# The norm's reciprocal root by Ln and Exp on ScalarE, in place of Sqrt on ScalarE and a reciprocal on VectorE

## Chip, cores and metric

The kernel runs on one core of a Trainium2 chip. The metric is the device time of one launch in microseconds, the median of the runs shown. The engines are called PE (TensorE), DVE (VectorE), ACT (ScalarE), POOL (GpSimd) and SP (SyncE, which only issues transfers here).

## What is computed

A layer of 2048 tokens and 1024 channels: a normalised input goes through a Mamba-2 block and, beside it, through a linear layer with a mixture of LoRA experts; both are added to the input. Cut to what matters:

```
xn = layernorm(x)
gate, hbc, dt = split(xn @ in_proj_w.T)
xBC = silu(causal_conv4(hbc))                  # x (64 heads of 64), B, C (8 groups of 128)
state = state * exp(dt * A) + (dt * x) B^T     # per token and head
y = state C + x * D
yg = y.reshape(L, 8 groups, 512)
var = mean(yg * yg, axis=-1)
yn = yg * rsqrt(var + 1e-5) * norm_weight * silu(gate)
out = x + yn @ out_proj_w.T + base(xn) + lora(xn)
```

The change is about `rsqrt(var + 1e-5)`.

## The kernel before

Channels lie on partitions. Tokens are cut into two spans `s` of 1024, each span into two halves of 512 (TB), each half into four chunks of 128 (Q). Large matrix products are done with one or two levels of Strassen's scheme in fp32: one pair of output tiles takes seven products of four 128x512 steps (`pair`, L450), in the order 1, 6, 5, 2, 7, 3, 4 on the PSUM tiles ps_a, ps_x, ps_y, ps_a, ps_x, ps_y, ps_x. Copies and sums between them (L474 and L529 on ACT; L478, L482 and L531 on DVE) take a partial result out of PSUM before the next product may add to the same tile. Product 7's eviction (L531) has to be done before product 4 starts, one product later.

After a start-up, a loop runs over 32 blocks (span, group, half) and in each over four chunks (L974 to L1069). It interleaves the scan with the projections: each chunk draws four or five of the seven products of a pair from a generator (`products`, L591), so that PE always has projection work between the steps of the scan. Matmuls keep their program order; the other engines' instructions are put in order by the framework's scheduler, and each engine then runs its list strictly in order. So an instruction that waits holds up all that stand behind it.

One chunk of the scan: `scan_a` makes the decay products `es` (L688, DVE), then C^T B and B^T (ps_cb), copied out as cbm and bt (L698, L700, ACT), the masked matrix dab (L702, DVE), then x transposed (ps_xt) and scaled to xdt (L713, eight ACT instructions) and xdd (L720, POOL). `scan_b` makes ps_y from xdt and dab, ps_e from the state, ps_st for the next state, and takes them out on DVE (L757 or L759, L760, L774). The tiles ps_cb, ps_xt and ps_nv share one PSUM bank, "aux".

In chunks 1 and 2 of a block, `conv` makes the next block's convolution: a first tap on ACT (L640), three more on DVE (L646), Silu on ACT (L653). Its output tile xg has two buffers, so the first L640 of the next block waits until the block before has stored its last result from the same buffer.

The norm of a block is spread over two blocks. In the last chunk `norm_squares` adds x * D (L793) and squares (L798, ACT). In the first chunk of the following block `norm_mean` (L804) sums over channels with a matmul by ones (ps_nv, L807), ACT takes Sqrt into the tile rms (L809), and `norm_gate` (L812) takes the reciprocal on DVE (L815), multiplies four slices by norm_weight and rms (L818), multiplies by the gate in two halves (L826) and stores each (L827, SP queue). There are 32 such norms.

In the first span, `small` (L297) makes the second span's dt, decay and router weights for four pieces of tokens, in between; its softplus is a chain of short DVE instructions (L319 to L326) that ends in `at` (L329, DVE), of which ACT takes Exp (`ex`, L330).

ACT's functions come from tables; the profile shows each switch as ACT_TABLE_LOAD, put down to the line of the instruction that needs it. Silu is used by L529 and L533 (gate) and L653, Exp by L315, L330, L338 and L385, Sqrt by L225, L268 and L809.

After the blocks comes the output projection with two levels of Strassen (from 2740 us on), in which ACT has little to do.

## Time and profile before

| | |
|---|---|
| Median of 3 runs | 3461.18 us (3456.09 to 3463.89) |
| The profiled execution's own time | 3459.94 us |
| Its span on the core | 3458.2 us |
| TensorE clock granted | 0.996 |
| Span under ACT's work in blocks | about the first 2700 us |

The profile's first part gives each engine's busy time as a share of the span. The waits give, for an engine and line, what released it, with the total in us, how often, and the longest. A group of instructions is told as line, engine, operation, tiles, shapes and count, then the busy time in us, the mean ns of one, and the idle time before it with its releaser. The chain that ended last is read from the end back: start, length, and what ran then; "issue" is time in which the engine waited for nothing that the profile shows, or in which the work of the line above goes on, as for the second piece of a long instruction.

The 40 slices of the span show where each engine works (tenths of each slice):

```profile
PE   9999999999999999999999999999999999999999
PEld 7444544544545554444555555444445588888888
DVE  7548787877887877677888887777885466566665
ACT  2223343333433333323333333333331000000000
```

### The profile page before, as it was taken

The page shows a single profiled execution, that of the slowest core. Times are in us where ns is not written, and L with a number is a line of the kernel's source. Part 1 is how long each engine was busy: PE and PEld are TensorE (multiplying, and loading weights), DVE is VectorE, ACT ScalarE, POOL GpSimd, SP SyncE. Part 2 cuts the span into 40 slices and gives each one's busy share as a digit, 9 for nine tenths or more (in the row PEclk, how much of TensorE's full clock was granted, in tenths as well). Part 3 has the DMA queues.
Part 4 walks back from the last instruction along what each step waited for, and adds up shares of the span by engine and source line. Part 5 has one row for each costly group of instructions (what it writes and reads, how often), then busy time and mean ns, then how long its engine had stood idle before and what let it go on. Part 6 is the DMA issues. An engine that isn't in the chain of part 4 may idle for free.

```text
span 3458.2 us, 37638 instructions
## 1 busy us (share of the span) xinstructions
PE 3409.4 (99%) x12818; PEld 1993.4 (58%) x12818; DVE 2530.2 (73%) x2861; ACT 926.4 (27%) x2158; POOL 832.3 (24%) x571
## 2 busy tenths in 40 slices
PE   9999999999999999999999999999999999999999
PEld 7444544544545554444555555444445588888888
DVE  7548787877887877677888887777885466566665
ACT  2223343333433333323333333333331000000000
POOL 3133323233333211332332433322332000000000
PEclk9999999999999999999999999999999999999999
DMA  6546655655656676787787788787777687585644
GB/s 234 189 164 201 209 178 189 206 191 197 199 193 205 197 262 220 246 283 231 240 251 245 234 260 253 234 255 226 244 233 270 236 279 242 198 299 188 213 165 145
DMA packets 530319, 769.79 MB, mean 223 GB/s; under 512 B 35152, under 2 KB 264656, under 8 KB 527440
## 3 DMA queue, kind: packets, MB, share of 16 engines
q1 hardware_dynamic: 530128, 767.39, 68.6%
q8 instruction: 102, 1.67, 0.2%
q14 instruction: 89, 0.73, 0.1%
HBM read 516.64 MB, written 250.61 MB: 222 GB/s over the span
## 4 chain that ended last, share of the span: by engine, by line
PE 77%; DVE 10%; issue 6%; DMA 4%; POOL 2%; ACT 1%; SPq 0%; POOLq 0%; DVEq 0%; ACTq 0%
PE ps_x_x L79 10%; PE ps_x_w L79 8%; PE ps_a_x L79 7%; PE ps_y_x L79 7%; PE ps_x_g L79 6%; PE ps_a_w L79 6%; PE ps_y_w L79 6%; PE ps_y_g L79 4%; PE ps_a_g L79 4%; PE ps_y L79 3%; PE ps_e L79 3%; PE ps_x_b L79 2%; PE ps_st L79 2%; PE ps_a_b L79 2%; PE ps_y_b L79 2%
## 5 line engine op out<-in xcount | busy, mean ns | idle before, releaser
L688 DVE TENSOR_TENSOR_SCAN es<-dab,here 128x1024 f32<-128x1024 f32 x128 | 327.3, 2557 | 285.8 <-POOL xdd L83 264.6
L83 POOL TENSOR_TENSOR xdd<-xdt,es 128x512 f32<-128x512 f32 x128 | 145.3, 1135 | 1003.4 <-ACT xdt L713 967.6
L646 DVE SCALAR_TENSOR_TENSOR xg<-rawx,cw,xg 128x512 f32<-128x512 f32 x384 | 339.8, 934 | 22.3 <-ACT xg L640 21.7
L79 PE MATMUL ps_x_w<-t,w 128*128 128x256 f32 x1344 | 303.8, 379 | 0.0
L79 PEld LDWEIGHTS ps_x_w<-t,w 128*128 128x128 f32 x1344 | 255.4, 190 | 41.5 <-issue 7.7
L713 ACT ACTIVATE xdt<-ps_xt,dt 128x64 f32<-128x64 f32 x1024 | 223.2, 331 | 201.4 <-PE ps_xt L88 201.4
L83 POOL TENSOR_TENSOR wo<-wo 128x512 f32<-128x512 f32 (+1 forms) x112 | 214.1, 1912 | 16.6 <-DMA ecp<-run_d 10.3
L83 POOL TENSOR_TENSOR state<-state,tot 128x512 f32<-128x512 f32 x112 | 134.5, 1201 | 322.4 <-PE ps_e L79 311.0
L79 PE MATMUL ps_a_w<-q,w 128*128 128x256 f32 x896 | 202.5, 379 | 0.0
L702 DVE TENSOR_TENSOR dab<-es,cbm 128x1024 f32<-128x1024 f32 x128 | 174.1, 1360 | 27.5 <-ACT cbm L698 27.4
L1336 ACT COPY s<-ps_a_w 128x512 f32<-128x512 f32 x28 | 16.4, 585 | 636.2 <-PE ps_a_w L79 568.9
L79 PEld LDWEIGHTS ps_a_w<-q,w 128*128 128x128 f32 x896 | 170.2, 190 | 23.6 <-issue 0.5
L79 PEld LDWEIGHTS ps_y<-dab,xdt 128*64 128x64 f32 x2048 | 114.0, 138 | 109.6 <-issue 72.6
L79 PE MATMUL ps_y_x<-op_again,s_x 128*128 128x512 f32 x384 | 173.3, 594 | 0.0
L79 PE MATMUL ps_x_x<-op_again,s_x 128*128 128x512 f32 x384 | 172.7, 592 | 0.0
L79 PE MATMUL ps_a_x<-op_again,a_x 128*128 128x512 f32 x384 | 172.7, 592 | 0.0
L79 PE MATMUL ps_x_x<-op,s_x 128*128 128x512 f32 x368 | 165.5, 592 | 0.0
L79 PE MATMUL ps_y_x<-op,s_x 128*128 128x512 f32 x368 | 165.5, 592 | 0.0
L79 PE MATMUL ps_a_x<-op,a_x 128*128 128x512 f32 x368 | 165.4, 592 | 0.0
L646 DVE SCALAR_TENSOR_TENSOR bc<-rawb,cw,bc 128x512 f32<-128x512 f32 x192 | 159.1, 859 | 4.0 <-ACT bc L640 3.2
L79 PE MATMUL ps_y<-dab,xdt 128*64 128x128 f32 x2048 | 145.9, 283 | 13.4 <-ACT xdt L713 13.4
L79 PE MATMUL ps_e<-bc,state 128*128 128x128 f32 x960 | 142.1, 292 | 0.0
(236 smaller groups left out, 6050.7 us busy)
## 6 DMA issues: line engine op xcount, KB each, us to landing
w<-w SPq DMA_DIRECT2D x196, 512.0 KB, 3.7
dab<-da_d SPq DMA_DIRECT2D x128, 512.0 KB, 5.1
raw<-ev SPq DMA_DIRECT2D x192, 256.0 KB, 3.2
a_x<-in_w_in_dram SPq DMA_DIRECT2D x168, 256.0 KB, 4.2
w<-wo SPq DMA_DIRECT2D x96, 448.0 KB, 3.5
ecp<-run_d SPq DMA_DIRECT2D x256, 128.0 KB, 4.0
gate<-ev SPq DMA_DIRECT2D x128, 256.0 KB, 3.5
sg<-gate SPq DMA_DIRECT2D x32, 1024.0 KB, 7.3
```

The source lines that it names most:

```text
L79: tc.keep_in_program_order(nc.tensor.matmul(*args, **kw))
L83: ins = nc.gpsimd.tensor_tensor(*args)
L646: nc.vector.scalar_tensor_tensor(dst[:, i, :], raw[:, i, k : k + TB], cw[:, ti, k : k + 1], dst[:, i, :], ALU.mult, ALU.add,)
L688: nc.vector.tensor_tensor_scan(es.rearrange("p h t -> p (h t)"), dab.rearrange("p h t -> p (h t)"), here, 0.0, ALU.mult, ALU.add,)
L702: nc.vector.tensor_tensor(ms, es, cbm.unsqueeze(1).to_broadcast([P, HG, Q]), ALU.mult)
L713: ins = nc.scalar.activation(xdt[:, h, :], x_t[:, h, :], AF.Copy, scale=dt_of[s][:, half * NQ + c, at : at + 1],)
L1336: nc.scalar.copy(s1, pa)
```

## The change

In `norm_mean` the ACT instruction computes Ln(var + eps) in place of Sqrt, from the same PSUM tile, with the same bias and scale. A second ACT instruction then computes Exp(-0.5 * that) in place in the tile rms, in SBUF. The reciprocal on DVE at the head of `norm_gate` is gone; its `yield` stays, so the following steps are handed out at the same points of the program. The other lines are the same; line numbers from L810 on move by one or two.

```diff
         std = p1.tile([P, TB], F32, tag="rms", name=f"rms_{s}_{g}_{half}")
-        nc.scalar.activation(std, ps, AF.Sqrt, bias=eps, scale=1.0 / (4 * P))
+
+        nc.scalar.activation(std, ps, AF.Ln, bias=eps, scale=1.0 / (4 * P))
+        nc.scalar.activation(std, std, AF.Exp, scale=-0.5)
         norm_of[s, g, half] = std
 
     def norm_gate(s, g, half):
 
         xg, std = xbc_of[s, g, half][0], norm_of[s, g, half]
-        nc.vector.reciprocal(std, std)
         yield
```

The two other places that take Sqrt and a reciprocal, the layer norms at L225 and L268, are left as they are. In the new file Ln is L810, Exp L811, and what was L818, L826 and L827 is L819, L827 and L828; the prediction uses the old numbers, except L811 for Exp.

## The prediction

> **What bounds the kernel now.** I read the page's first part (busy time by engine), then who waited for whom on TensorE (PE), then the groups that the change touches, then two stretches of the chain that ended last.

> ```profile
> PE 3409.4 (99%) x12818; PEld 1993.4 (58%) x12818; DVE 2530.2 (73%) x2861; ACT 926.4 (27%) x2158; POOL 832.3 (24%) x571
> ```

> PE is busy in all but 49 us of the 3458.2 us span. VectorE (DVE) and ScalarE (ACT), which the change edits, count only where PE stands still for them. PE's own waits (us, times, longest):

> ```profile
> PE ps_y L79 <- ACT xdt L713: 13.4, 5, 6.8
> PE ps_nv L79 <- ACT xdt L713: 10.0, 4, 2.7
> PE ps_st L79 <- POOL xdd L83: 5.4, 1, 5.4
> ...
> PE ps_x_g L79 <- DVE ev L531: 2.7, 4, 1.3
> PE ps_mean L79 <- DVE half L183: 1.7, 2, 1.5
> PE ps_x_x L79 <- DVE ev L531: 1.7, 4, 0.6
> ```

> The whole list sums to 43.5 us: the ceiling of any gain, 1.3%. ps_y behind xdt lies almost wholly at four places: PE starts ps_y at 451.69, 703.81, 955.68 and 1206.02 us, after gaps of 6.9, 1.5, 2.9 and 2.3 us (13.6). All four are in the first chunk after a norm, in blocks where small() computes `at` (L329) for the second half. The chain into the first gap:

> ```profile
> 433.70 0.07 DVE rms L815
> 433.77 3.12 issue
> ...
> 449.83 0.91 ACT L330
> 450.74 0.39 issue
> 451.13 0.05 ACT ex L330
> 451.18 0.17 issue
> 451.35 0.30 ACT xdt L713
> ```

> The reciprocal stands in this chain, and so does a table load ahead of ex: ACT works in order, so xdt waits for ex. The second kind of gap starts from the norm too, by way of its store:

> ```profile
> 770.01 0.04 DVE rms L815
> ...
> 782.79 4.92 DMA y<-xg
> ...
> 787.82 0.82 ACT xg L640
> ...
> 801.03 0.69 DVE ev L531
> ```

> Here the next convolution cannot begin (L640 overwrites the buffer) until y has been stored; its taps then delay the eviction L531, and PE starts ps_x_g at 801.76 after a gap of 1.6 us. The same chain stands behind gaps at 634.59 (1.7), 638.45 (0.9) and 1051.88 (0.7): 4.9 us with this one. The ps_nv waits (1584 to 2481 us) and the ps_st wait come from GpSimd's xdd and the squares of L793; no reciprocal is in their chains.

> **The change part by part.** Durations:

> ```profile
> L815 DVE RECIPROCAL rms<-rms 128x512 f32<-128x512 f32 x32 | 107.0, 3344 | 6.5 <-ACT rms L809 6.5
> L809 ACT ACT_TABLE_LOAD x31 | 39.8, 1283 | 0.5
> L809 ACT ACTIVATE rms<-ps_nv,eps 128x512 f32<-128x512 f32 x32 | 22.0, 687 | 47.7 <-PE ps_nv L79 47.4
> L315 ACT ACTIVATE u<-u 128x512 f32<-128x512 f32 x1 | 0.6, 631 | 1.6 <-DVE u L314 1.6
> ```

> Removed: 32 reciprocals x 3.344 = 107.0 us of DVE. Exchanged: 32 Sqrt for 32 Ln of the same form; no row has an Ln, I take Sqrt's 687 ns, so nothing. Added: 32 Exp on 128x512, 631 ns by the Exp row of L315: 20.2 us of ACT.

> Table loads are the open point. [...] The instruction lists of the two builds say otherwise: 31 of the 32 Exp have a load of their own directly ahead (the other comes just behind an Exp of L385), Ln has 32 where Sqrt had 31, and 3 loads of L330 and 1 of L533 fall away: 31 + 1 - 4 = 28 more, x 1.283 = 35.9 us. [...]

> ```profile
> 432.19 0.69 ACT L809 ACTIVATE rms<-ps_nv,eps 128x512 f32<-128x512 f32 x1
> 432.89 1.28 ACT L385 ACT_TABLE_LOAD   x1
> 434.19 0.20 ACT L385 ACTIVATE m_b<-m_b 128x2 f32<-128x2 f32 x1
> ```

> The load follows at 0.01 us and is followed at 0.02. [...]

> ACT's 56 us: the first copy behind Exp is cbm (L698), which needs ps_cb from PE. In the first half ps_nv ends 5.4 to 6.8 us ahead of ps_cb (339.55 to 345.49, for one), so load, Ln, load and Exp (3.9 us) are mostly done in ACT's idle time. Where Ln was late (1741.70, cbm at 1742.48) cbm slips 1.1 us, with 6 us to its next reader on PE. So nothing; without that cover, 32 x 1.9 = 61 us.

> DVE's 107 us: no PE time in itself; only the chains above turn it into time. New waits: L818 now waits for Exp, and in two blocks (norms at 432 and 939) one L818 stands ahead of L759. Behind it are L759, L760 and L774, whose PSUM banks PE wants a chunk later (some 20 us). The stores of L827 move up a few places in SP's queue past evictions, sum stores and weight loads; they also become ready sooner. Nothing for both. PE's order is the same in both builds.

> The store chains: at the norm of 769.98 Exp ends 771.9, and four L818, one eviction, L702 and two L826 from their rows end near 780 instead of 782.8; the other two norms lead by 4 to 4.7 us (1017.85, 595.41). The four gaps are 0.7 to 1.7: all vanish, -4.9. Bounds 0 and -4.9.

> The four ex gaps, from the new order:
> - At 432.88: Exp 434.9; DVE ends the second L826 near 444.0 (before 445.8). But ACT's list now has two L640 ahead of load and ex; they wait for the store, 444.0 + 4.6 = 448.6, then 1.5 + 1.3 + 0.3: xdt at 451.6, before 451.35. +0.3.
> - 688.96: `at` 701.1 (before 703.2), but a L640 (store lands 702.1) and the eviction L529 stand ahead of xdt: 703.3 for 703.46. -0.2.
> - 939.46: `at` 953.1 (before 955.1), then a load for L529 (1.3) and L529 (0.6): -0.1.
> - 1190.39: `at` 1202.7 (before 1205.4), store 1203.7, L640, L529: 1204.9 for 1205.67. -0.8.
> Together -0.8. If nothing took the place of the old wait, 3.3 + 1.5 + 2.9 + 2.3 = -10.

> Re-sorted DVE queue: taps (L646) now often stand ahead of L531 or L478. Thirteen evictions of product 7 already end within 0.1 us of PE's next use of the bank. PE's waits on such evictions are 4.4 us in 8 times, 0.55 each; I take 4 new ones, +2.2 (bounds -2 and +7).

> Sum: -4.9 - 0.8 + 2.2 = -3.5. The profiled execution took 3459.94 us (1.7 around its span); it is 1.2 below the median 3461.18, which becomes 3457.7; I say 3457.

> **The rivals.**
> - *The gain comes through* (0.25): ex and xdt follow `at` without a new wait, -10 - 4.9 = -15: 3446. For it: the reciprocal is in both chains. Against: the new ACT order.
> - *Slower, xdt behind the store* (0.19): in six blocks the new list puts L640 ahead of xdt, and L640 waits for y's store ("ACT xg L640 <- DMA y<-xg": 58.3 us in 20 times, 2.9 each). If the store lands after `at` by more than the 0.3 us of ex, all of it goes to ps_y: 6 x 2.9 = 17.4, less the 4.9: +12.5, 3474. Against: the sums above let the store land before or with `at`.
> [...]

> **How the numbers follow.** The likeliest, a small gain within the noise, 0.56, own range 3449 to 3466. Range 3443 to 3471 leaves out the far halves of the two rivals. About 0.2% (7 us) is what a measurement of this kernel tells from no change: faster means under 3454. Faster 0.29 (rival one and a tail), same 0.52, slower 0.19.

> **What would show it.** DVE busy near 2423, ACT near 982, 119 table loads for 91, each 1283 ns without a gap; no L815. Right if PE's waits on DVE evictions and half fall while ps_y behind xdt stays at 10 to 14 us. ps_y behind xdt near 4 is rival one; over 20, rival two. Wrong if PE's busy time itself changes, or a new wait (cbm, Exp, a weight load) shows on PE with over 5 us.

## The result, and the profile after

The changed kernel takes 3479.01 us (median of 6 runs, 3476.90 to 3480.49) where the kernel before takes 3460.32 beside it: ratio 1.0056, 95% interval 1.0046 to 1.0067. The change costs 0.56%, some 19 us. The prediction said 3457 and a range of 3443 to 3471; it had the wrong sign. Line numbers from here on are the changed kernel's, but in quotes of the prediction. The profiled execution has a span of 3475.1 us (before 3458.2).

Busy time by engine, on the page of the changed kernel:

```profile
PE 3414.9 (98%) x12818; PEld 1994.7 (57%) x12818; DVE 2442.8 (70%) x2829; ACT 981.3 (28%) x2218; POOL 841.2 (24%) x571
```

ACT is busy 55 us longer (981.3 for 926.4; 56.1 were costed), with 119 table loads, as foretold. DVE is busy 87 us less, not 107: other rows grew, as the taps L646 of xg from 934 to 957 ns. And PE itself is busy 5.5 us longer, on the same 12818 matmuls in the same order. That was one of the prediction's own signs of being wrong.

The rows of ACT's new pair, with the second's table load (busy, mean ns, idle before it):

```profile
L811 ACT ACT_TABLE_LOAD x31 | 39.8, 1283 | 0.6
...
L810 ACT ACTIVATE rms<-ps_nv,eps 128x512 f32<-128x512 f32 x32 | 22.0, 687 | 46.6 <-PE ps_nv L79 46.3
L811 ACT ACTIVATE rms<-rms 128x512 f32<-128x512 f32 x32 | 20.1, 630 | 0.3
```

Every unit price was right within a nanosecond. The loss is elsewhere. PE's waits (us, times, longest):

```profile
PE ps_y L79 <- ACT xdt L713: 13.4, 4, 5.7
...
PE ps_st L79 <- POOL xdd L83: 8.8, 4, 4.2
PE ps_x_g L79 <- DVE ev L531: 6.9, 5, 2.1
PE ps_x_x L79 <- DVE ev L531: 5.2, 4, 2.2
```

ps_nv behind xdt is 10.0 again. Against before, the wait for evictions L531 is 7.7 us up (12.1 for 4.4) and that for xdd 3.4 up (8.8 for 5.4); ps_y behind xdt is where it was. PE's wait for DVE's tile half (ps_mean) is 0.5 us instead of 1.7. With PE's own 5.5 us this makes 7.7 + 3.4 + 5.5 - 1.2 = 15.4 of the 16.9 us of span. None of these instructions was edited.

What changed around them is their order. Between the two builds, 328 of DVE's 2829 common instructions, 184 of SP's 2149, 28 of ACT's and 3 of POOL's lie outside the longest order that both lists share. The chain into the longest new wait, at 1237.94 us, in the changed kernel:

```profile
1222.64 2.35 DVE xg L646 x2
...
1225.68 0.68 DVE ev L531
1226.37 0.67 DVE xg L646
...
1227.09 0.37 SPq L622
...
1227.55 7.93 DMA a_g<-in_w_in_dram
...
1236.83 1.07 POOL xdd L83
1237.94 2.08 PE ps_st L79 x2
```

Read downwards: taps stand ahead of an eviction, SP's load of rawx (L622) waits for the last tap, a weight load (L423) for projection work waits behind it in SP's list and takes 7.93 us, POOL's sum for that weight stands ahead of xdd, and PE waits. Before, the same load stood ahead of rawx in SP's list:

```profile
1221.65 0.33 SPq L423 DMA_DIRECT2D a_g<-in_w_in_dram  x1
1224.11 0.37 SPq L621 DMA_DIRECT2D rawb<-raw  x1
1224.98 0.36 SPq L622 DMA_DIRECT2D rawx<-raw  x1
```

It landed 3.0 us after its issue, xdd started at 1228.15, and PE came to ps_st at 1231.32 without a wait. PE itself stands 3.0 us later in the changed kernel, so the load is 2.9 us later in issue (1227.55 for 1221.65, less 3.0) and 4.9 us longer in flight.

### The profile page after: what moved, and what is told of

Same layout as the page of the kernel before. It is cut to its first block, busy times and chain, and to the rows that moved or that the text cites. A ratio compares the mean times of both kernels' runs of the same rounds, so it can differ in the third digit from the quotient of the medians.

```text
span 3475.1 us, 37614 instructions
## 1 busy us (share of the span) xinstructions
PE 3414.9 (98%) x12818; PEld 1994.7 (57%) x12818; DVE 2442.8 (70%) x2829; ACT 981.3 (28%) x2218; POOL 841.2 (24%) x571
## 4 chain that ended last, share of the span: by engine, by line
PE 60%; DVE 4%; issue 2%; DMA 1%; POOL 1%; ACT 1%; SPq 0%; POOLq 0%; DVEq 0%; ACTq 0%
PE ps_x_w L79 8%; PE ps_x_x L79 6%; PE ps_a_w L79 6%; PE ps_y_w L79 6%; PE ps_x_g L79 5%; PE ps_y_x L79 4%; PE ps_a_x L79 4%; PE ps_a_g L79 3%; PE ps_y_g L79 3%; PE ps_x_b L79 2%; PE ps_e L79 2%; PE ps_y L79 2%; PE ps_st L79 2%; PE ps_a_b L79 2%; PE ps_y_b L79 2%
## 5 line engine op out<-in xcount | busy, mean ns | idle before, releaser
L83 POOL TENSOR_TENSOR xdd<-xdt,es 128x512 f32<-128x512 f32 x128 | 142.4, 1112 | 1017.4 <-ACT xdt L713 982.9
L646 DVE SCALAR_TENSOR_TENSOR xg<-rawx,cw,xg 128x512 f32<-128x512 f32 x384 | 350.8, 957 | 20.7 <-ACT xg L640 19.6
L79 PE MATMUL ps_x_w<-t,w 128*128 128x256 f32 x1344 | 303.8, 379 | 0.0
L713 ACT ACTIVATE xdt<-ps_xt,dt 128x64 f32<-128x64 f32 x1024 | 223.7, 332 | 205.0 <-PE ps_xt L88 205.0
L79 PEld LDWEIGHTS ps_x_w<-t,w 128*128 128x128 f32 x1344 | 255.4, 190 | 41.5 <-issue 7.7
L83 POOL TENSOR_TENSOR wo<-wo 128x512 f32<-128x512 f32 (+1 forms) x112 | 215.7, 1926 | 15.3 <-DMA ecp<-run_d 9.0
L83 POOL TENSOR_TENSOR state<-state,tot 128x512 f32<-128x512 f32 x112 | 142.9, 1276 | 311.4 <-PE ps_e L79 294.6
L79 PE MATMUL ps_a_w<-q,w 128*128 128x256 f32 x896 | 202.5, 379 | 0.0
L702 DVE TENSOR_TENSOR dab<-es,cbm 128x1024 f32<-128x1024 f32 x128 | 170.0, 1328 | 26.9 <-ACT cbm L698 26.9
L79 PEld LDWEIGHTS ps_a_w<-q,w 128*128 128x128 f32 x896 | 170.2, 190 | 23.6 <-issue 0.5
L79 PEld LDWEIGHTS ps_y<-dab,xdt 128*64 128x64 f32 x2048 | 114.9, 139 | 110.5 <-issue 65.0
L79 PE MATMUL ps_y_x<-op_again,s_x 128*128 128x512 f32 x384 | 173.3, 594 | 0.0
L79 PE MATMUL ps_x_x<-op_again,s_x 128*128 128x512 f32 x384 | 172.7, 592 | 0.0
L79 PE MATMUL ps_a_x<-op_again,a_x 128*128 128x512 f32 x384 | 172.7, 592 | 0.0
L79 PE MATMUL ps_x_x<-op,s_x 128*128 128x512 f32 x368 | 165.5, 592 | 0.0
L79 PE MATMUL ps_y_x<-op,s_x 128*128 128x512 f32 x368 | 165.5, 592 | 0.0
L79 PE MATMUL ps_a_x<-op,a_x 128*128 128x512 f32 x368 | 165.4, 592 | 0.0
L646 DVE SCALAR_TENSOR_TENSOR bc<-rawb,cw,bc 128x512 f32<-128x512 f32 x192 | 161.9, 874 | 4.0 <-ACT bc L640 3.2
L79 PE MATMUL ps_y<-dab,xdt 128*64 128x128 f32 x2048 | 146.7, 284 | 13.4 <-ACT xdt L713 13.4
L79 PE MATMUL ps_e<-bc,state 128*128 128x128 f32 x960 | 140.4, 290 | 0.9 <-ACT hw L405 0.6
```

Of the source, the lines that this page charges most:

```text
L79: tc.keep_in_program_order(nc.tensor.matmul(*args, **kw))
L83: ins = nc.gpsimd.tensor_tensor(*args)
L646: nc.vector.scalar_tensor_tensor(dst[:, i, :], raw[:, i, k : k + TB], cw[:, ti, k : k + 1], dst[:, i, :], ALU.mult, ALU.add,)
L702: nc.vector.tensor_tensor(ms, es, cbm.unsqueeze(1).to_broadcast([P, HG, Q]), ALU.mult)
L713: ins = nc.scalar.activation(xdt[:, h, :], x_t[:, h, :], AF.Copy, scale=dt_of[s][:, half * NQ + c, at : at + 1],)
```

## Experiments

Theory 1: the edits themselves are worth what was costed, or more, and the time is lost by the re-sorted lists. Theory 2: it is lost by ACT's added work and the later root. Theory 3: it is lost because DVE, earlier in each norm, moves transfers and evictions into each other, in whatever order.

To hold a list, a kernel gets, at its end, an edge of issue order between each instruction and the next of its engine, in the order wanted. No wait is added: where the change's own lists are held but for one load, the trace has 834 semaphore instructions on DVE, 516 on ACT and 1709 on SP, and the change has 834, 517 and 1709. With this the lists of one kernel can be given to the other (shortened):

```diff
+    for engine, moved in ORDER.items():
+        seq = [traced[engine][k + m] for k, m in enumerate(moved)]
+        for a, b in zip(seq, seq[1:]):
+            tc.add_manual_dep(b, a.name, no_sync, reason="order")
```

"Old order" is the lists of the kernel before, "new order" those of the changed kernel. All runs, each with 3457 to 3458 us for the kernel before beside it (3 lower than in the first comparison, so ratios are what to compare; 0.001 is 3.5 us):

| run | instructions, lists | us | ratio to before |
|---|---|---|---|
| the change | new, new | 3479.0 | 1.0056 (1.0046 to 1.0067) |
| new_instr_old_order | new, old | 3449.0 | 0.9976 (0.9968 to 0.9984) |
| old_instr_new_order | old, new | 3510.1 | 1.0155 (1.0142 to 1.0169) |
| new_instr_new_sync_order | new, SP and POOL new | 3468.7 | 1.0037 (1.0025 to 1.0050) |
| no_recip_old_order | no reciprocal, old | 3449.8 | 0.9978 (0.9970 to 0.9987) |
| recip_only_removed | no reciprocal, its own | 3466.2 | 1.0024 (1.0014 to 1.0034) |
| ln_exp_and_recip | Ln, Exp and reciprocal, its own | 3468.4 | 1.0033 (1.0021 to 1.0045) |
| new_weight_load_early | new, new but one load | 3470.0 | 1.0037 (1.0025 to 1.0049) |
| new_evictions_first | new, new but 40 evictions | 3484.3 | 1.0075 (1.0062 to 1.0088) |
| new_all_weight_loads | new, new but 106 loads | 3499.2 | 1.0115 (1.0102 to 1.0129) |
| new_loads_and_evictions | both of these | 3494.6 | 1.0104 (1.0091 to 1.0118) |
| new_sync_one_load_early | new, SP new but one load | 3458.4 | 1.0005 (0.9997 to 1.0013) |
| old_order_evictions_late | new, old but 39 evictions | 3487.3 | 1.0086 (1.0072 to 1.0100) |
| new_instr_softplus_first | new, old but four moves | 3445.9 | 0.9967 (0.9955 to 0.9979) |
| new_instr_ex_first | new, old but five moves | 3441.4 | 0.9951 (0.9938 to 0.9963) |
| old_instr_ex_first | old, old but five moves | 3450.2 | 0.9977 (0.9969 to 0.9986) |

### The lists and the instructions, crossed

**The changed kernel in the old order.**

> The changed kernel's instructions, each engine's list held in the order that the kernel before has (Exp directly behind its Ln, the reciprocal's place dropped). Theory 1, the re-sorted lists cost the time: the list order is worth about +17 us and the instructions themselves nothing or a few us of gain, so 3454 to 3461 us here. Theory 2, ScalarE's added 55 us and the wait for Exp cost it: the instructions are all still there, so 3474 to 3480. Theory 3, VectorE being 3.3 us earlier in each norm shifts transfers and evictions into each other: also 3470 to 3480.

Measured 3449.0, ratio 0.9976: the same instructions are faster than the kernel before by 0.24%, and faster than theory 1's range. The change and its lists part here: 0.0080, 28 us, lie in the order alone. PE's waits in this run:

```profile
PE ps_y L79 <- ACT xdt L713: 6.9, 5, 4.6
PE ps_st L79 <- POOL xdd L83: 4.9, 1, 4.9
...
PE ps_x_g L79 <- DVE ev L531: 1.4, 3, 0.6
PE ps_x_x L79 <- DVE ev L531: 0.9, 2, 0.6
```

ps_y behind xdt is halved (13.4 to 6.9), the evictions' wait is halved too (4.4 to 2.3). This is the gain that the prediction's first rival saw, at half to three quarters of its size (8.2 us by the medians, 11.1 by the spans, for 15).

**The kernel before in the new order.**

> The kernel before (Sqrt and reciprocal), each engine's list held in the order of the changed kernel, the reciprocal directly ahead of its first reader. Theory 1: 3474 to 3484 us, as slow as the changed kernel or a little slower, since VectorE also keeps its 107 us. Theory 2: 3458 to 3463, as before, since ScalarE has no added work. Theory 3: 3458 to 3463 too.

3510.1, ratio 1.0155: with not one added ACT instruction the new lists cost 53 us, which is 26 us over theory 1's range. They were made for a DVE that is 107 us less busy; with the reciprocal still there, PE waits 22.5 us for L531 and 18.0 for xdt (ps_y). So 53 us is not the price of the lists in the change. But in both lists the edit makes the kernel faster, by 0.0024 in the old and by 0.0099 in the new, and the new lists make it slower with both sets of instructions. As explanations of the loss, theories 2 and 3 fall.

**SyncE's and GpSimd's lists alone.**

> The changed kernel with VectorE's and ScalarE's lists in the old order, and only SyncE's (its DMA issues) and GpSimd's in the new one. Theory 1, by the offsets of the matched matmuls: the late load of a_g at 1231 us (about +6.6 of the 17) is SyncE's and stays, the evictions of product 7 behind the taps (about +8 to 10) are VectorE's and go: about 3464 to 3469 us. If VectorE's list carries all of it: 3455 to 3461. If SyncE's carries all of it: 3474 to 3480. Theories 2 and 3: 3470 to 3480.

3468.7, at the upper end of theory 1: SP's list (with three moves on POOL) costs 0.0061 (21 us) by itself, beside the old lists of DVE and ACT. PE waits 14.0 us for xdd there (4.9 in the old order) and 4.2 for half (0.4). DVE's and ACT's lists on top bring 0.0019 more; the two intervals overlap a little, so this part is small and its size uncertain.

**The relief alone.** L815 left out, Sqrt kept; the norm multiplies by the root instead of dividing by it.

> The kernel before without the reciprocal: the norm multiplies by the root itself, Sqrt stays on ScalarE, every list in the old order. What VectorE's relief is worth alone. Theory 1: 3453 to 3460 us (the gain that the prediction counted, up to 5.7 us, or nothing). Theory 2: the same, 3453 to 3460, so that the difference to the first run of this call is the price of ScalarE's added work. Theory 3: 3468 to 3480, since the relief itself does the harm.

3449.8, 3 us below theory 1's range. Leaving out the reciprocal is worth 7.4 us, and ACT's added work (58 us and 30 more table loads in this order: 986.1 for 928.4 us busy) costs nothing that can be measured (3449.0 with it). In this order the costing "so nothing" was right. No run has the new lists without that work, so its price there is not shown.

### What re-sorts the lists

The two halves of the change alone, each with lists of its own from the scheduler:

```diff
-        nc.vector.reciprocal(std, std)                      # recip_only_removed
...
-        nc.scalar.activation(std, ps, AF.Sqrt, ...)         # ln_exp_and_recip
+        nc.scalar.activation(std, ps, AF.Ln, ...)
+        nc.scalar.activation(std, std, AF.Exp, scale=0.5)
```

> One half of the change alone: Sqrt stays, the reciprocal is left out (the norm multiplies by the root itself), and the scheduler orders the lists anew. It moves 341 of 2829 DVE instructions against the kernel before (328 in the changed kernel, 173 of them differ between the two). If the relief of VectorE is what makes the scheduler re-sort, and re-sorting is the loss: 3465 to 3485 us, though the same edit in the old order took 3450. If the loss belongs to Ln and Exp in the scheduler's eyes: 3448 to 3460.

3466.2: the same edit, 3449.8 in the old order, loses 0.0046 (16 us) to its lists. So leaving out one DVE instruction of 3.3 us per norm is enough to re-sort 341 DVE instructions and turn a gain of 7 us into a loss of 8.

> The other half of the change alone: Ln, and Exp of plus half of it (so the tile holds the root), and the reciprocal kept on VectorE; the scheduler orders the lists anew. It moves 106 DVE instructions against the kernel before, where leaving out the reciprocal moved 341. If what costs is the re-sorting that follows from VectorE's relief: 3457 to 3465 us. If ScalarE's 55 us and the norm's later root cost by themselves: 3470 to 3485.

3468.4, between the two cases: a miss. With 106 DVE instructions and 80 of SP moved, and a root that comes later, it loses 0.0033. PE's wait for xdt goes from 13.4 to 14.7 and PE's busy time from 3409.4 to 3412.7 in its profile, whose span (3462.4) is short of the median. What of this is the later root and what the order was not separated.

### One transfer

In the new order, one load moved (entries of SP's list, not code):

```diff
   s_g_d<-s_g          L429   (issued 1220.32)
+  a_g<-in_w_in_dram   L423
   raw<-ev             L535   (1221.54)
   s_g_d<-s_g          L429
   raw<-ev             L535   (1226.39)
   rawx<-raw           L622
-  a_g<-in_w_in_dram   L423   (1227.55)
```

> The changed kernel in its own order, but for one transfer: the load of a_g that was issued at 1227.55 us stands four places further ahead in SyncE's list, directly behind the store of s_g at 1220.3. If that one late load makes the wait for xdd at 1237.94 (3.6 us) and the slow matmuls behind it (3.0 us): 6.6 us less than the changed kernel's 3479, 3470 to 3474. If another wait takes its place: 3477 to 3480.

3470.0; 0.0019 less than the change, 6.6 us, as expected, though the two intervals overlap a little. The place itself is clear: matched matmul by matmul, the step at 1237.94 is 3.6 us smaller, and the seven matmuls behind it, which ran at half the clock in the change, give 3.0 more.

The cleaner place is the run with SP's list new and the others old, where the same load goes back by one place only, ahead of rawx:

> The run with only SyncE's and GpSimd's lists in the new order (3468.7 us), but for the one load of a_g that was issued at 1224.39: it goes back ahead of the load of rawx, one place. If that place makes the wait of 7.8 us for xdd and the slow matmuls behind it: 8 to 11 us less, 3457 to 3461. If the load goes 0.5 us sooner and no more: 3467 to 3469.

3458.4; 0.0032 less, 11 us for one place of one DMA. Matched matmul by matmul, 10.2 us of the difference lie at this place. The views of L423 in the stretch from 1205 to 1230 us, first behind rawx, then ahead of it (in the second line of each, us from issue to landing):

```profile
L423 SPq DMA_DIRECT2D a_g<-in_w_in_dram x1: 457/457/457, 1224.4 to 1224.4; - x1
...
DMA to landing us min/median/max: 8.8/8.8/8.8
```

```profile
L423 SPq DMA_DIRECT2D a_g<-in_w_in_dram x1: 383/383/383, 1218.9 to 1218.9; - x1
...
DMA to landing us min/median/max: 2.8/2.8/2.8
```

The load pays twice: it is issued 5.5 us later, since rawx waits 4.6 us for the last tap, and it then needs 6.0 us more: issued 0.5 us behind the 1 MB of rawx, it lands 0.6 us behind it (1233.2 for 1232.6). This is no single case: in the traces of the kernel before and of the change, a load L423 is issued directly behind a rawx, by 0.42 to 0.56 us, in 9 and in 8 places. In all 17 it lands 0.63 to 0.73 us behind rawx, 6.9 to 9.2 us after its own issue; on both pages the median for a_x, one of the tiles that L423 loads, is 4.2 us.

### The evictions

In the new order, 40 evictions L531 moved ahead of taps that the old order has behind them (entries of DVE's list):

```diff
+  ev<-ps_x_x,s_x   L531
   xg<-rawx,cw,xg   L646
   ...
-  ev<-ps_x_x,s_x   L531
```

> The changed kernel in its own order, but for 40 evictions of L531 on VectorE that the new list has behind convolution taps (L646) and the old one ahead of them: each is moved ahead of those taps, 1 to 6 of them. If the taps ahead of the evictions cost the 9.8 us by which PE's waits for L531 exceed those in the old order, and the slow matmuls behind them (about 1.3): 3467 to 3472 us. If the next matmuls then wait for something else: 3476 to 3480.

3484.3, if anything slower still (the intervals overlap): a miss. The waits for L531 do fall, from 12.1 to 4.0, but those for xdd rise:

```profile
PE ps_st L79 <- POOL xdd L83: 21.1, 5, 10.7
```

The later taps free rawx later, and the a_g load at the place above is issued at 1245.78 and lands after 9.05 us; PE waits 10.7 us there. So one list can't be mended without the other.

The reverse, in the old order: 39 evictions put behind the taps.

> The changed kernel's instructions in the old order (3449 us), but for 39 evictions of L531 put behind the convolution taps that the new list has ahead of them (1 to 5 taps each). The reverse of the run that moved them forward inside the new order. If those taps cost what PE's waits for L531 show (12.1 against 2.3 us) and some slow matmuls: 3457 to 3463. If in this order the evictions have room: 3449 to 3453.

3487.3, 0.0110 (38 us) more than the old order: the direction of theory 1, at about three times the size expected. PE waits 28.7 us for L531, and is 12.7 us longer busy. The chain into one of these waits:

```profile
1987.05 4.01 DVE xg L646 x3
...
1993.27 0.73 DVE xg L646 x2
...
1995.25 0.61 DVE ev L531
...
1995.91 1.22 PE ps_x_x L79
```

So taps ahead of evictions can cost the whole loss by themselves, in this order. In the changed kernel the waits for L531 rose by 7.7 us.

### All weight loads

> The changed kernel in its own order, but every weight load (L423) in SyncE's list that the new order has behind transfers which the old one has behind it is moved ahead of them again: 106 loads, most by 1 to 7 places, 5 by 18; they pass stores of y (L828), of evictions (L535) and loads of raw (L625, L626). If weight loads held up behind stores and raw loads are SyncE's whole part (19.7 us where the other lists were old): 3459 to 3465 us. If the one load at 1227.55 was all of it: 3468 to 3473, as in the run that moved it alone (3470).

3499.2, 20 us slower: a miss. One wait for xdd of 22.2 us stands at 1502.68. Five loads had been moved ahead by 15 to 18 places there; they are issued one by one from 1466.61 to 1477.69, and what they passed comes after them: the stores of s_b_d (L857) at 1478.71 instead of 1462.56, the loads of wo that wait for these, and ecp at 1491.47 instead of 1470.80. POOL's sums and xdd stand behind. Without this place (a step of 18.0 us) it would be some 2 to 5 us over the change's own time, where SyncE's part was to come back. A load moved ahead that itself waits holds up the rest of the list.

> The same 106 weight loads moved ahead, and the 40 evictions moved ahead of the taps (alone they cost 5 us: their own waits fell by 8.1 us, but the waits for xdd rose by 12.3). If xdd rose because weight loads stood behind transfers that wait for the taps, then with the loads free the 8 us come: 5 to 9 us less than the run with the loads alone. If the evictions do harm in another way: the same as that run or slower.

3494.6, 0.0011 (4 us) less, which is within the noise of both. In the two traces the offsets of the matched matmuls fall by 7 us, chiefly at the evictions from 1650 to 2555 us (-1.7, -2.3, -2.3, -1.6), and xdd takes some back. So this run decides between its two cases only by its trace, and the same place at 1502 is still in it.

### What is left in the ex chains

In the old order, the last 6 to 11 short softplus instructions (L319 to L329) go ahead of the norm's slices, in four places; in the second run L533 also goes behind the eight xdt at the first place (entries of the lists of DVE, then ACT):

```diff
   dab<-es,cbm   L702   (DVE)
+  po, dt, at    L323 to L329
   xg<-xg,nw,rms L819
   ...
-  po, dt, at    L323 to L329
...
-  ev<-ev        L533   (ACT)
   ex<-at        L330
   xdt<-ps_xt,dt L713 x8
+  ev<-ev        L533
```

> The changed kernel's instructions in the old order (3449 us), but for four places in which the last 6 to 11 short DVE instructions of the softplus chain (L319 to L329) are moved ahead of the norm's slices (L819, L827) that stand in between. PE's wait there is 6.9 us (ps_y behind xdt). If that wait hangs on the chain behind the slices: 5 to 7 us less, 3442 to 3445, the wait under 2 us. If the slices, now 2 to 3.5 us later, make the stores and the next convolution late: 3447 to 3452.

3445.9, 3 us less, between the two cases and within the noise of both runs. PE's wait did not fall: three places give 1.9, the first one loses 2.5, since ACT's L533 waits for an eviction until 449.05 (ps_y behind xdt 7.5 for 6.9). What the 3 us are in the trace is PE's busy time, 3404.8 for 3408.3.

> As the run with the softplus chain ahead of the norm's slices (3446 us), and at the first of its four places ScalarE's list also has the Silu of the gate (L533, which waits there for an eviction of VectorE until 449.05) behind ex and the eight xdt instead of ahead. There PE waited 7.1 us for xdt. If that one instruction was what held ex: 6 to 7 us less, 3438 to 3441 us, and ps_y behind xdt under 1.5 us. If xdt then waits for its own data: 3443 to 3446.

3441.4, at the edge of the first case. ps_y behind xdt is 1.3 us in all, and this is the fastest kernel of all runs here: ratio 0.9951 to the kernel before, 0.0105 (36 us) under the change.

> The kernel before (Sqrt and reciprocal) in its own order, with the two moves that brought the changed kernel's instructions from 3449 to 3441 us: the softplus chain ahead of the norm's slices in four places, and one L533 behind xdt. If the gain of the moves is independent of the change: 3446 to 3452 (8 to 10 us under before), and the change is worth 5 to 9 us on top. If the change's own gain at the old order was just these ex chains, the moves take it over: 3441 to 3446.

3450.2, 0.9977, as in the first case: the moves are worth 8 us without the change as well, and the change another 0.0026 (9 us) on top. So its own gain at a held order does not hang on the ex chains alone. With ps_y at 1.2 and 1.3 us, the traces show that gain at xdd (7.5 to 5.4), at L531 and half (6.4 to 2.8) and in PE's busy time (3407.9 to 3404.2).

## Why the prediction was wrong, step by step

PE's waits and busy time in us, from the profiles:

| | before | the change | new, old order | old, new order |
|---|---|---|---|---|
| ps_y behind xdt | 13.4 | 13.4 | 6.9 | 18.0 |
| ps_x_g and ps_x_x behind L531 | 4.4 | 12.1 | 2.3 | 22.5 |
| ps_st behind xdd | 5.4 | 8.8 | 4.9 | 8.6 |
| ps_mean behind half | 1.7 | 0.5 | 0.4 | 0.7 |
| PE busy | 3409.4 | 3414.9 | 3408.3 | 3434.2 |
| span | 3458.2 | 3475.1 | 3447.1 | 3513.1 |
| mean granted clock | 0.996 | 0.995 | 0.996 | 0.991 |

- **Reciprocal, Ln, Exp, loads:** right, in count and price. In the change's trace Exp ends 1.94 us after Ln in 26 of the 32 norms, 2.04 in one and 3.92 in five; the sums took 1.9 for all. That ACT's work costs PE nothing is right with the old lists held.
- **The store chains, "all vanish, -4.9":** with the old lists held, three of the four gaps are gone. The fourth, at 638.45, was misread: it ends with ACT's L253 of the layer norm, and PE's wait there stands in every run, with 0.6 us in all but one. In the change half fell by 1.2 us, and the two gaps before L531 (1.3 and 0.5 us at 801.76 and 1051.88 before) are still there with 1.0 and 0.8.
- **The ex gaps, "together -0.8":** the total held (ps_y 13.4 and 13.4), and in ACT's list L640, L529 and a load do stand ahead of xdt, as was said. But the four places moved by -1.1, +1.1, +0.1 and +0.4 us, where +0.3, -0.2, -0.1 and -0.8 were forecast. At the first, xdt is 0.7 us later, and PE waits less only because PE itself comes 1.8 us later. That the sum came out is in part luck. In the old lists the same edit gives -6.5.
- **"Re-sorted DVE queue: ... I take 4 new ones, +2.2 (bounds -2 and +7)":** this term failed. PE's waits for L531 rose by 7.7 us, over the upper bound. It was the price and not the count: 9 waits for 8 before, but 1.3 us each in place of 0.55, and up to 2.2. An average of past waits was no measure for new ones.
- **"The stores of L827 move up a few places in SP's queue ... Nothing for both":** this failed too, and by the run that splits the lists it is the larger part: 21 us for SP's and POOL's, some 7 more for DVE's and ACT's on top. SP's list was taken as a few stores further ahead; 184 of its entries had moved, and one weight load behind rawx made 6.6 us of the change, as its own run shows. xdd was not in the sum at all, though "a weight load" with over 5 us was named as a sign of being wrong.
- **PE's busy time** was taken as fixed. Its 5.5 us come with the new stalls (below).
- **The rivals.** "The gain comes through", -15, is what the edits do in the old lists (-8.2 by the medians, -11 by the spans). "Slower, xdt behind the store", 3474, had nearly the time, but not the mechanism: ps_y behind xdt did not rise.

In one line: the sum had -0.8 for ps_y and -4.9 + 2.2 for the store chains and evictions, and nothing for xdd and PE's busy time. Measured were 0.0 for ps_y, +6.5 for L531 and half, +3.4 for xdd and +5.5 for PE's busy time, 15.4 of the 16.9 us of span.

So the edits were costed well, and the re-sorting was counted only at the places where the edits were. What stays open: how the 28 us divide over the moves of the new lists, since the parts do not add up (evictions alone make it no better, one load alone does), and what SyncE's other moves are made of. With the load put back they still cost 0.0029 (10 us), which goes with waits for half (4.4 us, 0.4 in the old order) and L531 (5.9, for 2.3).

## What to carry to other kernels

Where a scheduler orders the lists, an edit has two effects, and the second can be several times the first: count how many instructions change places on every engine, the DMA issuer included, and hold the old order to measure the edit itself. Look in the new lists for an eviction behind work that PE doesn't wait for, and for a weight load behind a transfer that waits. If the edit wins with the order held, keep the order held.

## What was not expected of the hardware

A stall cost PE more than its own time here. In the run with late evictions, around the wait that ends at 1995.91 us (columns: stretch, length, busy time of PE, PEld, DVE, ACT, POOL with instructions, granted clock, DMA share, GB/s):

```profile
1985.00:1992.00 7.00, 7.00 (x19) 2.99 (x17) 7.00 (x8) 3.12 (x5) 6.76 (x5) 1.00 0.44 173
1996.00:2000.00 4.00, 4.00 (x5) 1.76 (x6) 3.19 (x5) 0.00 (x0) 0.00 (x0) 0.50 1.05 296
2000.00:2004.00 4.00, 4.00 (x11) 1.82 (x10) 0.69 (x1) 0.95 (x5) 0.00 (x0) 0.78 0.83 257
```

The granted clock is at one half from 1994.97 to 2001.79 us, and the matmuls of 128x512 start every 0.85 instead of 0.43 us until then. That is 5.9 us behind PE's restart, of which 2.9 are lost, so the stall of 3.8 us costs 6.8.

In the traces of the kernel before and of the change, of 22 gaps of PE between 0.45 and 1.9 us none was followed by a clock under 0.9 in the next 3 us, of 15 between 1.9 and 2.9 us 7 were, the shortest of them 2.11 us long, and of 7 longer ones all.

So PE's busy time grew with its waits in these runs. PE worked at half clock for 20.7 us in the kernel before, 28.7 in the change, 19.9 in the old order and 41.6 with late evictions; half of the differences is 4.0 of the change's 5.5 us, and 10.8 of the 12.7 us that late evictions add to PE's busy time, beside 26 us of waits.
